# Experts' tiles laid out in pairs of one expert, with the up products made by seven half-size products

## The chip, the cores and the metric

The kernel runs on one core of one Trainium2 chip. A core has five engines with an instruction queue each: TensorE (PE; its weight loads are shown apart as PEld), VectorE (DVE), ScalarE (ACT), GpSimd (POOL) and SyncE (SP, which only issues transfers). Each engine takes its queue in order. The metric is the device time of one execution in microseconds (us), lower is better. A profiled execution has a span (from its first to its last instruction) that is a little shorter than its device time.

## The reference

A layer of gated attention and a mixture of experts over x of 2 x 2048 tokens of 512 numbers, all float32:

```python
xn = layernorm(x)
s  = attn(xn)              # causal, one head of 512, with its own norm and residual
# experts: 8, two per token, D = 512, H = 352
scores = xf @ gate_w.T + gate_b + bias
top_scores, top_idx = top_k(scores, 2)
gates = softmax(top_scores)
h = silu(einsum('td,ehd->teh', xf, w1) + b1)
y = einsum('teh,edh->ted', h, w2) + b2
out = sum over the token's two experts of gate * y
return x + s * silu(out)
```

The kernel computes an expert only for the tokens that chose it: 2 x 4096 = 8192 rows of work in all.

## The kernel before

The program has three stages, all in one order written out by hand (each engine runs its instructions in the order of the calls).

**First** (to about 258 us): the norm, the keys and values, and the routing. `route()` counts each expert's rows on DVE and gives each row a place in a list of 68 tiles of 128 rows (`NS`). The first 57 tiles (`FULL`) hold rows of one expert only; the last 11 are split into two halves of 64 rows, each of its own expert. `first`, `behind`, `end`, `jump` (L562 to L587) are the arithmetic of this layout; `toki` says which token stands in which place (L644), `posi` where a token's two rows went, `eidi` the expert of each tile or half (L663), `b1sel` its bias (L666 to L676). The pools of the expert stage are opened when `route()` has ended.

**Second** (about 259 to 599 us): the experts, one tile per call of `experts_step(i)` (L941). A tile i passes through these calls, spread over several steps so that each has time:

- `gather` (L773): POOL issues an indirect transfer of the tile's 128 rows from DRAM (`xs`), five tiles ahead.
- `turn` (L842): SP issues a transfer that transposes them (`xhT`), three tiles ahead; `join` (L847): DVE puts the two 16-bit halves of each number together again (`xT`), one tile ahead.
- `up` (L881): PE multiplies by w1 of the tile's expert; the expert's number is read into a PE register. Four products over the four chunks of D, each 128 x 352; a float32 product is two records in the profile.
- `turn_h` (L895): ACT scales the result (`h`), POOL separates its halves (`hu`), SP issues the transposing transfer (`huT`).
- `join_h` (L906): DVE joins the halves (`ht`), ACT adds the bias and applies silu in three pieces. Called two steps later.
- `down` (L919): PE multiplies by w2, three products of 512 columns, called three steps later; `keep_y` (L934), one step after that: DVE copies the result out of PSUM, SP stores it (`y_d`).

For the split tiles, `copy_w1` (ACT, L867) and `copy_w2` (DVE, L872) first copy the second half's weights to `w1c` and `w2c`, since a product takes one register. From step 8 to 46, every second step also lets SP issue one of 20 transfers that the attention will need (`early`: 16 of keys, 4 of queries; L1117 to L1121), and the last of them is followed by `query_sums(0)` on POOL.

**Third** (to the end): the attention, two rows of tiles at a time where it can. There, scores and values of some pairs are already made by seven products of half-size blocks in place of eight, with sums and differences of blocks made by DVE and POOL (`fast_scores`, `values_first`, `values_next`, `values_end`). `gather_y` and `gate` (L1347) fetch the two expert rows of each token, weigh them (ACT, DVE) and apply silu (ACT). At the last step, `gate(NT - 2)` stands between `values_next` and `values_end` (L1530), and `make_ahead` (L1379) uses its result.

Of the kernel before, what the change touches and what calls it, by code (L numbers as in the profile page):

```python
# [20 lines left out]
P = 128  # L21
# [5 lines left out]
def gated_attention_moe(  # L27
# [26 lines left out]

    nc = tc.nc
# [14 lines left out]

    HALF = P // 2
    FULL = -((E * (P - 1) - 2 * NT * P) // P)
# [3 lines left out]
    assert HL < P and HL % 32 == 0 and D == 512 and TB == 512  # L76

# [367 lines left out]
    def route():  # L445

        with ExitStack() as rt:
# [28 lines left out]
            full = counting("full", NT, step=P)  # L476

# [18 lines left out]
            def best(scores, k):  # L496
# [43 lines left out]

            count = rp.tile([P, E, 1], F32, name="count")
# [4 lines left out]
            nc.vector.tensor_scalar(short, count, 1.0 - P, None, ALU.add)  # L546
# [4 lines left out]
            halves = rp.tile([P, 2, E, 1], F32, name="halves")  # L551
            nc.vector.tensor_reduce(halves[:, 0, :, 0], more, AX.X, ALU.add)
            nc.vector.tensor_scalar(halves[:, 0], halves[:, 0], 2.0, None, ALU.mult)
            rest = rp.tile([P, E, 1], F32, name="rest")
            nc.vector.scalar_tensor_tensor(
                rest, halves[:, 0], -float(HALF), count, ALU.mult, ALU.add
            )
            nc.vector.tensor_scalar(halves[:, 1], rest, 0.0, None, ALU.is_gt)
            nc.vector.scalar_tensor_tensor(
                halves[:, 1], rest, float(HALF), halves[:, 1], ALU.is_gt, ALU.add  # L560
            )
            behind = rp.tile([P, 2, E, 1], F32, name="behind")  # L562
            nc.vector.tensor_tensor_scan(
                behind.rearrange("p k e o -> p (k e o)"), ones[:, : 2 * E],
                halves.rearrange("p k e o -> p (k e o)"), 0.0, ALU.mult, ALU.add,
            )
            first = rp.tile([P, 2, E, 1], F32, name="first")
            nc.vector.tensor_tensor(first, behind, halves, ALU.subtract)

# [5 lines left out]
            end = rp.tile([P, E, 1], F32, name="end")  # L575
            nc.vector.tensor_scalar(end, behind[:, 0], float(HALF), None, ALU.mult)
            jump = rp.tile([P, E, 1], F32, name="jump")
            nc.vector.scalar_tensor_tensor(
                jump, first[:, 1], float(HALF), end, ALU.mult, ALU.subtract
            )  # L580
            nc.vector.tensor_tensor(
                excl, excl, cum.rearrange("p (e t) -> p e t", e=E), ALU.add
            )
            nc.vector.tensor_tensor(excl, excl, shift.to_broadcast(G), ALU.add)
            nc.vector.tensor_tensor(more, excl, end.to_broadcast(G), ALU.is_ge)
            nc.vector.tensor_tensor(more, more, jump.to_broadcast(G), ALU.mult)
            nc.vector.tensor_tensor(excl, excl, more, ALU.add)  # L587

# [264 lines left out]
    def places(i):  # L855

        if i < FULL:
            return [(slice(0, P), i)]
# [736 lines left out]
```

## Time and profile before

| | us |
|---|---|
| median of 3 runs | 1049.39 (1048.91 to 1050.32) |
| the profiled execution | 1049.65 |
| its span | 1047.9 |
| PE busy in the span | 1037.7 |
| DVE busy | 635.8 |
| POOL busy | 435.4 |
| ACT busy | 332.5 |
| mean granted TensorE clock | 1.000 |

The page of the profile gives the busy time of each engine, then the span in 40 slices, then the chain of waits that ended last, then the groups of instructions by line. In a group's row, the numbers are the count, the busy time in us and the mean of one in ns, and behind the bar the idle time of the engine just before them with what ended it. PE's records are pipelined: a record's own length includes the way through the array, so the pace of a row of products is read from the distance of their starts, as the chain of waits gives it (so many records in so many us), and not from the mean length. The timeline gives start, length, engine, line and operation of each instruction; a bracket behind it is the idle time before it and what ended it. SPq is the queue of SP's transfers, and a landing is not shown in it: it is read from the instruction that waited for it.

### The profile page before, as it was taken

Reading aid. Unit: us, or ns where it says so; the run is one execution under the profiler, and the core shown is the slowest. Engines: PE = TensorE matmul, PEld = TensorE weight load, DVE = VectorE, ACT = ScalarE, POOL = GpSimd, SP = SyncE. Lnnn points to the kernel's source line nnn. Section 1 sums busy time; section 2 is a strip of 40 time slices with the busy share of each in tenths; the row PEclk is TensorE's granted clock in tenths of the full one; section 3 lists DMA queues with packets and bytes.
Section 4 is the critical chain, followed back from the end, with each engine's and each line's share of the span. In section 5 each row is a group of like instructions: output and inputs, shape, how many; then the busy total and the mean of one; then the engine's idle time right before and its main releaser. Section 6 shows DMA issues by size and latency. Waiting matters only on the chain.

```text
span 1047.9 us, 12221 instructions
## 1 busy us (share of the span) xinstructions
PE 1037.7 (99%) x3566; PEld 617.6 (59%) x3566; DVE 635.8 (61%) x1195; ACT 332.5 (32%) x675; POOL 435.4 (42%) x469
## 2 busy tenths in 40 slices
PE   9999999999999999999999999999999999999998
PEld 5687886444555555555545446776764544447577
DVE  5787884775433333333335558787556556788676
ACT  3222222211332232223246323222334553542340
POOL 2364150003433333334332117444656777764272
PEclk9999999999999999999999999999999999999999
DMA  8699999956999999999889257635767868754361
GB/s 299 186 285 283 272 266 329 333 177 172 203 228 224 229 224 230 224 232 227 201 192 169 70 191 171 136 91 131 189 176 232 259 186 230 184 144 120 96 159 40
DMA packets 300513, 209.34 MB, mean 200 GB/s; under 512 B 234520, under 2 KB 247576, under 8 KB 299424
## 3 DMA queue, kind: packets, MB, share of 16 engines
q1 hardware_dynamic: 280960, 145.60, 57.0%
q0 software_dynamic: 10560, 35.17, 13.2%
q10 hardware_dynamic: 8928, 27.79, 7.5%
q8 instruction: 30, 0.49, 0.2%
q14 instruction: 35, 0.29, 0.1%
HBM read 92.89 MB, written 60.03 MB: 146 GB/s over the span
## 4 chain that ended last, share of the span: by engine, by line
PE 89%; DVE 3%; issue 3%; POOL 2%; ACT 1%; DMA 1%; SPq 0%; ACTq 0%; POOLq 0%; DVEq 0%
PE py L928 16%; PE ph L889 15%; PE ps L1002 13%; PE p L1245 10%; PE p L1054 8%; PE po L1197 7%; PE p L402 7%; PE pj L343 3%; PE pw L209 3%; PE pj L348 3%; PE p L1197 2%; DMA zuT<-zu 1%; ACT w1c L870 1%; PE pg L309 1%; POOL xs L775 1%
## 5 line engine op out<-in xcount | busy, mean ns | idle before, releaser
L928 PE MATMUL py<-w,ht 128*128 (+3 forms) x408 | 186.6, 593 | 0.0
L889 PE MATMUL ph<-w,xT 128*128 (+1 forms) x544 | 173.1, 460 | 0.7 <-POOL keep L1111 0.7
L936 DVE COPY y<-py 128x512 f32<-128x512 f32 x68 | 46.9, 690 | 177.4 <-PE py L928 173.8
L914 ACT ACTIVATE ht<-ht,b1sel 128x128 f32<-128x128 f32 (+3 forms) x237 | 73.1, 375 | 222.3 <-DVE ht L908 220.3
L1002 PE MATMUL ps<-k,q 128*128 128x512 f32 (+3 forms) x416 | 143.0, 495 | 0.0
L889 PEld LDWEIGHTS ph<-w,xT 128*128 128x128 f32 (+1 forms) x544 | 97.4, 181 | 74.1 <-issue 35.2
L899 POOL COPY hu<-h 128x704 uint16<-128x704 uint16 x68 | 52.6, 773 | 203.4 <-ACT h L897 111.4
L1157 POOL COPY pu<-pT 128x1024 uint16<-128x1024 uint16 (+2 forms) x74 | 82.1, 1141 | 117.0 <-ACT pT L1147 53.4
L928 PEld LDWEIGHTS py<-w,ht 128*128 128x128 f32 (+3 forms) x408 | 73.6, 182 | 78.0 <-issue 39.3
L1002 PEld LDWEIGHTS ps<-k,q 128*128 128x128 f32 x416 | 74.7, 190 | 67.6 <-issue 58.6
L775 POOL DMA_INDIRECT xs<-zu_d,toki x68 | 68.9, 1013 | 69.3 <-DVE toki L644 57.9
L1342 POOL DMA_INDIRECT yg<-y_d,posi x64 | 68.3, 1067 | 38.1 <-DVE yg L1353 22.7
L1197 PE MATMUL po<-v,pT 128*128 128x512 f32 x182 | 81.1, 592 | 0.0
L266 POOL COPY zu<-z 128x1024 uint16<-128x1024 uint16 x32 | 35.2, 1100 | 78.3 <-DVE z L251 78.3
L1179 DVE COPY pT<-puT 128x1024 uint16<-128x1024 uint16 (+2 forms) x74 | 55.0, 774 | 6.1 <-DMA puT<-pu 6.1
L1197 PEld LDWEIGHTS po<-v,pT 128*128 128x128 f32 x182 | 34.2, 190 | 38.1 <-issue 36.4
L415 DVE TENSOR_TENSOR so<-p,so 128x512 f32<-128x512 f32 x70 | 45.8, 685 | 15.7 <-DMA v_d<-so 9.3
L849 DVE COPY xT<-xhT 128x1024 uint16<-128x1024 uint16 x68 | 47.4, 697 | 10.5 <-PE ph L889 5.8
L1147 ACT ACTIVATE pT<-pT,nm 128x1024 f32<-128x1024 f32 x14 | 16.1, 1149 | 111.3 <-DVE nm L1090 72.2
L1363 DVE SCALAR_TENSOR_TENSOR o<-xo,xscale,o 128x512 f32<-128x512 f32 x30 | 28.8, 967 | 33.2 <-ACT o L1360 32.0
L1147 ACT ACTIVATE pT<-ps,nm 128x512 f32<-128x512 f32 (+3 forms) x52 | 30.0, 581 | 58.8 <-DVE nm L1090 36.7
L1060 DVE TENSOR_TENSOR pT<-p,pT 128x512 f32<-128x512 f32 x49 | 32.9, 686 | 25.9 <-PE p L1054 18.7
(248 smaller groups left out, 1713.2 us busy)
## 6 DMA issues: line engine op xcount, KB each, us to landing
y_d<-y SPq DMA_DIRECT2D x68, 256.0 KB
zu_d<-zu SPq DMA_DIRECT2D x32, 264.0 KB
kt_d<-kT ACTq DMA_DIRECT2D x8, 1024.0 KB
k<-kt_d SPq DMA_DIRECT2D x32, 256.0 KB
q<-qt_d SPq DMA_DIRECT2D x32, 256.0 KB
v<-v_d SPq DMA_DIRECT2D x32, 256.0 KB
xo<-in_x_dram SPq DMA_DIRECT2D x32, 256.0 KB
x<-in_x_dram SPq DMA_DIRECT2D x30, 256.0 KB
```

Source lines behind the costliest of these rows:

```text
L402: nc.tensor.matmul(ps[:, r, :], lhsT=lhs[:, c, ts(r, P)], rhs=rhs[:, c, :], start=(c == 0), stop=(c == 1),)
L775: nc.gpsimd.indirect_dma_start(out=xs, out_offset=None, in_=zu_d, in_offset=bass.IndirectOffsetOnAxis(ap=toki[:, i : i + 1], axis=0),)
L889: nc.tensor.matmul(ph[at, :], lhsT=xT[:, c, at], rhs=rhs[k], start=(c == 0), stop=(c == ND - 1),)
L914: nc.scalar.activation(ht[:hn, c, at], ht[:hn, c, at], AF.Silu, bias=b1sel[:hn, c, j : j + 1])
L928: nc.tensor.matmul(py[at, :], lhsT=ht[:k, c, at], rhs=rhs[n], start=(c == 0), stop=(c == NH - 1),)
L1002: nc.tensor.matmul(ps[:, :w], lhsT=aqs[seq[s] // 2][:, c, ts(t % 2, P)], rhs=aks[first + j][:, c, :w], start=(c == 0), stop=(c == ND - 1),)
L1054: nc.tensor.matmul(ps, lhsT=x[:, c], rhs=y[:, c], start=(c == 0), stop=(c == ND // 2 - 1))
L1157: nc.gpsimd.tensor_copy(pu[:, : 2 * w].rearrange("p (h d) -> p h d", h=2), turned[s][:, k : k + w].bitcast(U16).rearrange("p (d h) -> p h ...
L1179: nc.vector.tensor_copy(turned[s][:, k : k + w].bitcast(U16).rearrange("p (i t h) -> p i t h", t=P, h=2), puT[:, : 2 * w // P, :].rearrang ...
L1197: nc.tensor.matmul(dst, lhsT=turned[s][:, ts(k, P)], rhs=avs[first + k // BT][:, k % BT, cols], start=(start and k == k0), stop=(k == k1 - 1),
L1245: nc.tensor.matmul(dst, lhsT=a[:, k], rhs=v(k), start=(k == 0), stop=(stop and k == n - 1))
L1342: nc.gpsimd.indirect_dma_start(out=y, out_offset=None, in_=y_d, in_offset=bass.IndirectOffsetOnAxis(ap=posi[k][:, n : n + 1], axis=0),)
```

## The change

**The layout.** An expert's rows are first cut into pairs of full tiles, then into single full tiles, then into at most one or two halves. The numbers of each are fixed: 26 pairs (52 tiles), 60 full tiles in all in place of 57, 8 split tiles in place of 11, 68 tiles as before. `route()` works with three kinds (pairs, whole tiles, halves) where it had two.

```diff
-    FULL = -((E * (P - 1) - 2 * NT * P) // P)
+    PAIRS = (2 * NT * P - E * 3 * HALF) // (2 * P)
+    FULL = (2 * NT * P - E * HALF) // P
...
+    AHEAD_OF_PAIRS = 6
+    order = list(range(2 * PAIRS, 2 * PAIRS + AHEAD_OF_PAIRS)) + list(range(2 * PAIRS))
+    order += list(range(len(order), NS))
+    paired = range(AHEAD_OF_PAIRS, AHEAD_OF_PAIRS + 2 * PAIRS)
...
+            full2 = counting("full2", NT // 2, step=2 * P)
...
+            later = [more, sc2]
+            for k, past in enumerate(later):
+                nc.vector.tensor_tensor(past, excl, end[:, k].to_broadcast(G), ALU.is_ge)
+                nc.vector.tensor_tensor(past, past, jump[:, k].to_broadcast(G), ALU.mult)
+            for past in later:
+                nc.vector.tensor_tensor(excl, excl, past, ALU.add)
...
-            for k in range(2):
+            for k in range(3):
                 nc.vector.tensor_tensor(
                     ge, half.unsqueeze(1).to_broadcast(GS), first[:, k].to_broadcast(GS), ALU.is_ge
                 )
                 n = rp.tile([P, NJ], F32, name=f"begun{k}")
                 over_e(n, ge, ALU.add)
...
+            eid = begun[0]
+            for n in begun[1:]:
+                nc.vector.scalar_tensor_tensor(eid, n, 0.0, eid, ALU.is_equal, ALU.mult)
+                nc.vector.tensor_tensor(eid, eid, n, ALU.add)
```

Steps 0 to 5 run six single full tiles; steps 6 to 57 are 26 calls of `pair_step`; steps 58 and 59 are full tiles, 60 to 67 the split ones.

**The sums.** `w1_sums` makes four differences of blocks of w1 (176 columns by half of D) for all experts, two experts at a time after each of the steps 1 to 4: three on DVE, one on POOL, 704 numbers per partition each. `x_sums` makes the four sums of a pair's rows on DVE, 256 numbers each.

**The products.** `up_pair` makes the pair's `h` (256 x 352) from seven products of 128 x 176, each over two chunks of 128, with seven additions on DVE that read the products from PSUM, and one copy by ACT.

```diff
+    def w1_sums(e, parts):
...
+        for i, x1, x2 in (1, b12, b11), (2, b22, t[0]), (3, b22, b12), (4, b21, t[1]):
+            if i in parts:
+                engine = nc.gpsimd if i == 3 else nc.vector
+                engine.tensor_tensor(t[i - 1], x1, x2, ALU.subtract)
...
+    def x_sums(i):
+        q = wsp.tile([P, 3, ND // 2, P], F32, name=f"xs4_{i}", tag="xs4")
...
+        for dst, x1, x2, op_ in (
+            (s1, a21, a22, ALU.add), (a21, a11, a21, ALU.subtract),
+            (s2, s1, a11, ALU.subtract), (s4, a12, s2, ALU.subtract),
+        ):
+            nc.vector.tensor_tensor(dst, x1, x2, op_)
...
+        def made(x, y):
+            ps = ps_a.tile([P, TB], F32, name="p7", tag="a")[:, :H2]
+            for c in range(ND // 2):
+                nc.tensor.matmul(
+                    ps, lhsT=x[:, c], rhs=y(c).rearrange("p o h -> p (o h)"),
+                    start=(c == 0), stop=(c == ND // 2 - 1),
+                )
+            return ps
...
+        nc.scalar.copy(c11, made(a11, b(0, 0)))
+        meanwhile()
+        p2 = made(a12, b(1, 0))
+        add(c12, made(s2, t(2)), c11)
+        add(c11, p2, c11)
+        add(c21, made(s3, t(3)), c12)
+        p5 = made(s1, t(1))
+        add(c22, p5, c21)
+        add(c12, p5, c12)
+        add(c12, made(s4, b(1, 1)), c12)
+        add(c21, made(a22, t(4)), c21)
```

**The steps.** A pair's step does two tiles' work in one order; `keep_y`'s copies go to ACT there. `turn_h` of a paired tile scales `h` where it lies.

```diff
+    def pair_step(i):
+        keep_y(i - DOWN - 1, nc.scalar.copy)
+        gather(i + FIRST)
+        turn(i + 3)
+        turn(i + 4)
+        up_pair(i, lambda: join_h(i - 2))
+        turn_h(i)
+        gather(i + FIRST + 1)
+        turn_h(i + 1)
+        join_h(i - 1)
+        down(i - DOWN)
+        keep_y(i - DOWN, nc.scalar.copy)
+        down(i - DOWN + 1)
+        for k in range(i + 2, i + 4):
+            join(k)
+        if i + 2 in paired:
+            x_sums(i + 2)
```

In `experts_step`, which the other tiles keep, `copy_w1` is called before `turn_h` and not after it, and for split tiles `join_h` after `turn_h` and not before `up`:

```diff
-        at(join, 1)
-        at(join_h, -2)
+        if i + 1 not in xts:
+            at(join, 1)
+        if i < FULL:
+            at(join_h, -2)
         at(up, 0)
+        at(copy_w1, 1)
         at(turn_h, 0)
-        at(copy_w1, 1)
+        if i >= FULL:
+            at(join_h, -2)
         at(down, -DOWN)
```

**Pools and transfers.** The sums' memory (`wsp`) lies where the attention's keys and queries, `w1c` and `w2c` come later; these pools are opened at step 58. So the 20 early transfers are issued two at a time after the steps 58 to 67. The two PSUM pools are opened so that a tile waits only for the former user of its own place. `xT` has four buffers and `h` four (two each before).

```diff
-    ps_b = psum(att, name="ps_b", bufs=3)
-    ps_a = psum(att, name="ps_a", bufs=5)
+    ps_b = psum(att, name="ps_b", bufs=3, reuse_waits="tile")
+    ps_a = psum(att, name="ps_a", bufs=5, reuse_waits="tile")
...
-        if i >= 8 and i % 2 == 0 and early:
-            f, b, c = early.pop(0)
-            f(b, c)
-            if not early:
-                query_sums(0, nc.gpsimd)
+        if i < paired.start:
+            if 0 < i <= E // 2:
+                w1_sums(2 * (i - 1), (1, 2, 3, 4))
+            if i + 1 == paired.start:
+                join(i + 2)
+                x_sums(i + 1)
+        for _ in range(2):
+            if i >= paired.stop and early:
+                f, b, c = early.pop(0)
+                f(b, c)
+                if not early:
+                    query_sums(0, nc.gpsimd)
```

**The end.** At the last step of the attention, `gate` is moved into `values_end`, behind its joins and sums:

```diff
             values_next(s - 3)
-            gate(s - 1)
             values_end(
-                s - 3, [lambda: join_p(s)] * len(halves[s]) + [lambda: combine_p(s - 1)]
+                s - 3,
+                [lambda: join_p(s)] * len(halves[s])
+                + [lambda: combine_p(s - 1), lambda: gate(s - 1)],
             )
```

## The prediction

> **What bounds the kernel now.** I read the page's busy times first, then the chain of waits, then the timeline and the window table of the expert stage, since the change lies there.
>
> ```profile
> PE 1037.7 (99%) x3566; PEld 617.6 (59%) x3566; DVE 635.8 (61%) x1195; ACT 332.5 (32%) x675; POOL 435.4 (42%) x469
> ```
>
> PE is busy throughout at full clock, so work taken from PE is worth its time unless something else comes due. The chain of waits (start, length, what) through full tiles:
>
> ```profile
> 301.13 2.37 PE ph L889 x8
> 303.50 2.58 PE py L928 x6
> 306.08 2.37 PE ph L889 x8
> ```
>
> Nothing but products: 2.37 us for up (8 records of 352 columns, 0.2956 each) and 2.58 for down, 4.945 us a tile. The split tiles are different:
>
> ```profile
> 563.57 0.53 ACT h L897
> 564.10 1.26 ACT w1c L870
> 565.41 2.29 PE ph L889 x13
> ```
>
> Here ACT's copy of the second expert's weights, queued behind silu and `h`, ends last before each up. A step takes up to 5.4 us.
>
> **Pairs: PE.** Two ups cost 16 x 0.2956 = 4.73 us. A pair's seven products are 7 x 2 chunks x 2 records = 28 records of 176 columns. No row has 176. The pace is 0.2956 at 352 columns (above) and 0.216 at 256 (12 records in 2.59 us, line L1245 of the chain). Both fit columns x 0.833 ns + 2.3 ns, so 176 give 0.149. This needs the weight loads to keep up:
>
> ```profile
> 785.56 0.86 PEld L1002 LDWEIGHTS ps<-k,q 128*128 128x128 f32 x7 [0.24 <-issue]
> ```
>
> That is PE's loads ahead of products with only 128 columns. A load is 190 ns long, but seven start within 0.86 us, (0.86 - 0.19) / 6 = 0.112 each: they overlap. So 0.149 stands (bounds 0.149 and 0.190): 28 x 0.149 = 4.17, 0.556 less per pair, **26 x 0.556 = -14.5 us**. A pair's step is then 4.17 + 2 x 2.58 = 9.33 us.
>
> The Trainium skill (TensorE: Matmul & The Clock Gate, section "LDWEIGHTS") gives a load as its columns / 1.2 ns, 107 ns for 128. By that figure the loads need 3.0 us a pair and products decide; by the recorded 190 ns they would need 5.32 us and the change would lose. The measured pace of 0.112 is on the page's side.
>
> **Pairs: the others in 9.33 us.** DVE: two joins 0.70, two of `ht` 0.56, seven additions from PSUM (256 columns take 0.42 us, 128 take 0.29: 0.34), four sums of 256 columns (0.42): 1.40 + 1.12 + 2.38 + 1.68 = 6.6 us. ACT: two result copies 0.585 (row L353, same shape), the first product's copy 0.35, two `h` 0.53, two silus 0.98: 4.5. POOL: two gathers 1.1 and two `hu` 0.77: 3.7. SP: four transposes 1.3, two stores 0.5: 6.2. All fit. PSUM has five places for products; the sixth product needs the first's, which ACT has long copied.
>
> DVE and POOL get in each other's way, however. Alone, the sum of query blocks on L1023 takes 0.41 us; its mean is higher:
>
> ```profile
> L1023 DVE TENSOR_TENSOR sq<-q 128x256 f32<-128x256 f32 x5 | 5.3, 1057 | 0.0
> ```
>
> The long ones lie beside POOL copies or sums. The Trainium skill (SBUF — State Buffer, section "SBUF: two separate sides") has it that a DVE operation with two SBUF inputs and a POOL operation that reads SBUF take turns on one shared pair of ports, the later one waiting for the whole of the other. By that rule the two `hu` copies cost DVE up to 1.5 us a pair, 8.1 in all. From the rows alone I add nothing here and keep the long sums for a rival.
>
> Transfers: the pair moves what two tiles moved. In the windows of 0.2 us between 500 and 505 us the DMA engines are well below full in about six of 25, so a tile needs some 3.8 us of them, 7.7 a pair.
>
> **The loop through the transpose.** What could come due is a ring. DVE's `join_h(i-2)` stands ahead of the pair's additions and waits for `huT`, which left after the former pair's additions:
>
> ```profile
> 262.39 0.77 POOL L899 COPY hu<-h 128x704 uint16<-128x704 uint16 x1 [2.26 <-ACT h L897]
> 263.19 1.21 SPq L903 DMA_TRANSPOSE huT<-hu  x1
> ...
> 267.57 0.56 DVE L908 COPY ht<-huT 128x768 uint16<-128x768 uint16 x1 [2.77 <-DMA huT<-hu]
> ```
>
> From SP's issue to DVE it took 4.4 us. Around the ring: join 0.56, six additions 2.2, `h` 0.53, `hu` 0.77, transfer 4.4, hand-overs 0.3 = 8.8 us, 0.6 below 9.33. I take no stall; the other end is one blocked POOL copy and a transfer 0.5 later, 9.9. Every 0.1 us beyond 9.33 costs 2.6 us in all.
>
> **The split stage.** Eleven steps run from 533.55 to 592.17, 58.6 us. After: three full ones (14.8), three at 5.2 as the first three in the chain (where 64- and 128-row tiles alternate), five at 4.95, since the weight copy now starts at the end of up and needs 0.24 + 1.36 us while down takes 2.58: 54.8 to 55.2. **-3.4** (other end -1.2: only three splits less at 0.38). Silu, now behind `h`, ends about 4.1 us after up; down needs it at 4.95.
>
> The 20 early transfers move here, two a step, on SP behind `huT` and ahead of the next step's store and transpose: SP 3.2 + 2 x 0.57 = 4.3 of 5 us. At the 390 GB/s that some windows of 0.2 us show, 0.5 MB take 1.3 us, which the one step's lead of the joins covers; without it, silu's margin of 0.8 is gone. The query transfers of step 66 leave some 4.5 us after up(66), and the first scores start 7.6 after it (2.58 + 2.37 + 2.58); three us for landing leave nothing. **+0.5** (0 to 2). `query_sums(0)` moves on POOL from step 46 to 67, needed 20 us later, free.
>
> **The start.** `route()` gains ten small DVE operations before L604, 2.7 us; DVE then waits 2.5 us at 210 us for PE, which has other products to run, so nothing comes of it. After `toki` a third comparison (0.8 + 1.2) and two more steps for `eid` (0.24 each) add 2.4 us to what ends here:
>
> ```profile
> 249.87 2.33 DVE L673 SCALAR_TENSOR_TENSOR b1sel<-ge,b1s,b1sel 128x79 f32<-128x79 f32 x7
> ...
> 255.80 0.69 DVE L849 COPY xT<-xhT 128x1024 uint16<-128x1024 uint16 x1 [3.61 <-DMA xhT<-xs]
> ```
>
> SP's first transpose starts at 252.42, right behind it. The first `xT` would be there at 258.9 and not 256.5. PE's former products end at 258.36, and today up starts at 259.08 (after ACT's last copy out of PSUM, 258.98, which the finer PSUM waits remove): 0 (-0.5 to +1).
>
> `w1_sums` put 3 x 0.89 = 2.7 us (704 columns at 1.04 ns + 0.15) on DVE in each of four steps that hold 1.95 us already, 4.6 of 4.95, and a POOL difference of 1.9 us (L1371: 1.39 at 512) that DVE takes turns with. `join` is queued behind. By hand I get 0.4 us late at up(4) and 0.6 at the first `x_sums`; with each POOL operation blocking DVE once, about 1 us more in two or three steps. **+3** (1 to 6).
>
> **The end.**
>
> ```profile
> 1011.73 3.85 DVE L1353 SCALAR_TENSOR_TENSOR yg<-yg,share,yg 128x512 f32<-128x512 f32 x2 [4.23 <-DMA yg<-y_d,posi]
> ...
> 1015.96 2.86 PE L1245 MATMUL p<-vT,pT 128*128 128x256 f32 x12 [1.40 <-DVE u L1262]
> ```
>
> DVE waits in `gate` for rows from DRAM, and PE for the additions behind it. Moved, PE loses its 1.40 us wait. `make_ahead` and what follows on DVE come 2 to 3 us later; the additions at 1033.97 then run at about 1036.5, before PE needs them (1039.38, now 1038). **-1.4** (0 to -1.4).
>
> **Sum:** -14.5 - 3.4 + 0.5 + 3 - 1.4 = -15.8. The span 1047.9 becomes 1032.1; with 1.75 us around it 1033.9; the runs' median lies 0.26 below the profiled execution: 1033.6, I say **1033.5 us**.
>
> **Rivals.** *The ring decides.* For it: 0.6 us of slack only, and it keeps its delay once late. Against: the 4.4 us were taken with gathers in the way already. At 9.65 a pair, 26 x 0.32 = +8.3: about 1042 us.
>
> *DVE becomes the bound*, the slower side. Place: the pair's four sums and two joins beside POOL. If each sum takes the 1.4 us of the long ones (the median on L1022 and L1023), DVE needs 6.6 + 3.9 = 10.5 us a pair: 26 x 1.17 = +30, 1064 us. It costs the whole gain from 9.33 + 15.8 / 26 = 9.94 us on. Against: POOL reads SBUF for only 1.5 us a pair.
>
> *The loads don't overlap enough* and the pair saves nothing on PE: 28 x 0.190 = 5.32 in place of 4.17, 26 x 1.15 = +30, 1063 us. It loses from 0.1689 us a record (4.73 / 28), set the other terms aside. Against: 0.112 above.
>
> **Chances.** What the kernel's runs can tell from no change is about 0.2%, 2 us. Pairs bound by products (1030 to 1038): 0.60. The ring between 9.4 and 9.9 (1038 to 1047): 0.22. DVE as the bound: 0.11. Loads: 0.03. No difference by an accident of sizes: 0.03. Below 1030: 0.01. So faster 0.83, same 0.03, slower 0.14. Range 1029.5 to 1045: the forecast's terms at their kinder ends, and most of the ring's case.
>
> **What would show it.** Right: in the chain a pair as 28 records in 4.17 us and twice 2.58, without DVE, ACT or a transfer between. The ring: DVE's `ht` row idle on `huT`, then PE idle on DVE's additions. DVE as bound: its busy share near 1 there, the sums' mean above 0.9 us. Loads: records 0.17 to 0.19 apart with no wait named. The start: PE waiting for `xT` or the sums between 268 and 284 us. The splits: `w1c` gone from the chain. The end: no PE wait of 1.4 us near 1015. I am wrong altogether if a pair takes more than 9.94 us.

## The result, and the profile after

| | before | after |
|---|---|---|
| runs | 14 | 14 |
| median, us | 1049.21 | 1055.12 |
| shortest to longest, us | 1047.6 to 1052.4 | 1042.8 to 1068.0 |
| the profiled execution, us | 1049.65 | 1049.76 |
| its span, us | 1047.9 | 1048.1 |

The ratio after to before is 1.000, with a 95% interval of 0.998 to 1.002: no difference, where 1033.5 us had been forecast. The ratio leaves out runs more than 1.5% above a kernel's shortest one, here six of the fourteen, all above 1058 us; as these may well be this kernel's own, medians and extremes of all runs stand beside the ratios below. The profiled execution is one of the shorter runs, 5.4 us under the median; what is read from its trace explains that run.

The page's busy times say that the change did remove PE's work, and that the time didn't follow:

```profile
PE 1027.8 (98%) x3836; PEld 643.9 (61%) x3836; DVE 735.2 (70%) x1449; ACT 367.2 (35%) x741; POOL 461.7 (44%) x474
```

PE is busy for 9.9 us less in a span that is 0.2 us longer: it waits for 10 us more than before. The chain of waits through the first pairs shows both sides of it (start, length, what):

```profile
299.49 1.16 DVE ht L1005
300.66 1.18 DVE xT L875
...
303.87 3.25 PE p L968 x20
307.12 5.15 PE py L1025 x12
312.27 4.18 PE p L968 x28
316.45 5.16 PE py L1025 x12
```

Where nothing holds it, a pair is what was forecast: 28 records in 4.18 us, down in 5.16. Up to the second pair (303.87) the chain isn't on PE at all but goes through a landing and DVE's joins. The table of PE's waits in the expert stage (for whom, us in total, times, longest):

```profile
PE p L968 <- DVE xs L949: 2.5, 5, 1.0
PE ph L915 <- DVE xT L875: 2.3, 2, 1.8
PE ph L915 <- issue: 2.1, 1, 2.1
PE p L968 <- DVE h L975: 0.9, 2, 0.6
PE ps L1122 <- DMA q<-qt_d: 0.8, 1, 0.8
PE p L968 <- DVE xT L875: 0.4, 1, 0.4
```

Before, the same table has a single row, 0.7 us ahead of up(0). And DVE, which PE waits for, waits itself, in the pairs from 300 to 540 us, for the transposing transfers:

```profile
DVE ht L1005 <- DMA huT<-hu: 24.6, 22, 2.5
DVE xT L875 <- DMA xhT<-xs: 19.3, 17, 2.9
```

Set side by side from one marked point to the next, the two profiled executions differ like this:

| stretch | before, us | after, us | difference | forecast |
|---|---|---|---|---|
| to the last copy of the projections (ACT, 258.39 and 262.64) | | | +4.25 | 0 |
| from there to up(0) (259.08 and 264.67) | 0.69 | 2.03 | +1.3 | start: +3 |
| up(0) to the seventh tile (281.19 and 291.80) | 22.1 | 27.1 | +5.0 | (in the +3) |
| the next 52 tiles, which are the pairs now (to 538.77 and 540.45) | 257.6 | 248.65 | -8.9 | -14.5 |
| the rest to the first scores (592.10 and 592.04) | 53.3 | 51.6 | -1.7 | -2.9 |
| to the end of the span | 455.8 | 456.1 | +0.3 | -1.4 |
| sum | | | +0.2 | -15.8 |

The first row I take as not the change's: PE waits there for `zT`, before the routing, 1.9 us in the profile before and 4.1 after, and in the profiles of the kernels below that pause was anything up to 4.2 us, whatever they changed behind it. The others are the change's.

**The start.** Timelines of SP, DVE, PE and POOL:

```profile
258.99 6.77 SPq L870 DMA_TRANSPOSE xhT<-xs  x4
...
263.77 1.37 DVE L875 COPY xT<-xhT 128x1024 uint16<-128x1024 uint16 x2 [5.00 <-DMA xhT<-xs]
...
264.67 11.40 PE L915 MATMUL ph<-w,xT 128*128 x32 [2.06 <-issue]
...
277.59 2.30 POOL L938 TENSOR_TENSOR w1s<-w 128x704 f32<-128x704 f32 x1
...
278.28 2.15 DVE L875 COPY xT<-xhT 128x1024 uint16<-128x1024 uint16 x1
...
280.49 2.63 PE L915 MATMUL ph<-w,xT 128*128 x8 [1.85 <-DVE xT L875]
```

SP's first transpose leaves at 258.99, right behind the routing's last DVE operation, though its gather was issued at 243; then PE's first up waits. In the steps with sums of weights, `join` (0.69 us alone) takes 2.15 beside POOL's difference, and up waits for it: 1.85 us here, and the two steps behind take 5.65 us each, not 4.95.

**The pairs.** The timeline where the ring is set back:

```profile
380.34 5.87 SPq L870 DMA_TRANSPOSE xhT<-xs  x2
...
383.12 0.77 POOL L996 COPY hu<-h 128x704 uint16<-128x704 uint16 x1 [4.09 <-issue]
...
385.35 0.89 DVE L1005 COPY ht<-huT 128x768 uint16<-128x768 uint16 x1 [2.54 <-DMA huT<-hu]
386.17 0.68 DVE L875 COPY xT<-xhT 128x1024 uint16<-128x1024 uint16 x1
386.26 2.71 SPq L1000 DMA_TRANSPOSE huT<-hu  x2
...
389.30 0.86 PE L968 MATMUL p<-w1s,xs 128*128 x4 [0.51 <-DVE xs L949]
...
390.26 4.07 SPq L870 DMA_TRANSPOSE xhT<-xs  x2
...
391.65 0.56 DVE L1005 COPY ht<-huT 128x768 uint16<-128x768 uint16 x1 [1.95 <-DMA huT<-hu]
392.12 2.34 DVE L975 TENSOR_TENSOR h<-p,h 128x176 f32<-128x176 f32 x7
...
392.51 0.86 PE L968 MATMUL p<-w1s,xT 128*128 x4 [0.56 <-DVE h L975]
```

Two xhT transposes hold SP for 5.87 us; huT, queued behind them, leaves at 386.26 although `hu` was ready at 383.9, and DVE joins it at 391.65, 7.8 us after `hu`. DVE waits for `huT` ahead of the joins and of the seven additions, and PE waits for both. In the next pair the same order starts late.

**The end.** The timelines of DVE and PE:

```profile
1025.35 1.41 DVE L1490 SCALAR_TENSOR_TENSOR yg<-yg,share,yg 128x512 f32<-128x512 f32 x2
...
1033.30 0.42 DVE L1399 TENSOR_TENSOR o<-p,p 128x256 f32<-128x256 f32 x1
...
1033.78 1.99 PE L1334 MATMUL p<-v,pT 128*128 128x256 f32 x8 [1.67 <-DVE o L1399]
```

PE's wait of 1.40 us at 1015.96 is gone. A new one of 1.67 has come at 1032: PSUM has three places for these products, and the one that PE needs next comes free with an addition that now stands behind the gate and `make_ahead` on DVE.

### The profile page after: what moved, and what is told of

The parts are those of the page before. It is cut to its first block, busy times and chain, and to the rows that moved or that the text cites. A ratio compares the mean times of both kernels' runs of the same rounds, so it can differ in the third digit from the quotient of the medians.

```text
span 1048.1 us, 13294 instructions
## 1 busy us (share of the span) xinstructions
PE 1027.8 (98%) x3836; PEld 643.9 (61%) x3836; DVE 735.2 (70%) x1449; ACT 367.2 (35%) x741; POOL 461.7 (44%) x474
## 4 chain that ended last, share of the span: by engine, by line
PE 73%; issue 8%; POOL 7%; DMA 7%; DVE 4%; SPq 1%; ACT 0%; POOLq 0%; DVEq 0%
PE ps L1122 13%; PE py L1025 9%; PE p L1174 8%; PE p L1382 8%; PE p L412 8%; PE po L1334 7%; PE p L968 7%; PE pj L353 3%; PE pw L219 3%; PE pj L358 3%; PE p L1334 2%; POOL xs L801 2%; DMA huT<-hu 2%; POOL hu L996 1%; DMA zuT<-zu 1%
## 5 line engine op out<-in xcount | busy, mean ns | idle before, releaser
L1025 PE MATMUL py<-w,ht 128*128 (+3 forms) x408 | 182.2, 593 | 0.0
L996 POOL COPY hu<-h 128x704 uint16<-128x704 uint16 x68 | 63.7, 937 | 175.1 <-issue 129.6
L801 POOL DMA_INDIRECT xs<-zu_d,toki x68 | 75.1, 1105 | 69.5 <-DVE toki L669 57.8
L875 DVE COPY xT<-xhT 128x1024 uint16<-128x1024 uint16 x68 | 61.8, 916 | 25.2 <-DMA xhT<-xs 25.0
L975 DVE TENSOR_TENSOR h<-p,h 128x176 f32<-128x176 f32 x182 | 56.1, 337 | 15.2 <-PE p L968 8.0
L1005 DVE COPY ht<-huT 128x768 uint16<-128x768 uint16 x68 | 40.3, 592 | 33.2 <-DMA huT<-hu 31.4
L1508 POOL TENSOR_TENSOR o<-o,yg 128x512 f32<-128x512 f32 x30 | 41.4, 1381 | 14.9 <-DVE o L1500 14.7
```

The lines of the kernel that those rows point to most:

```text
L801: nc.gpsimd.indirect_dma_start(out=xs, out_offset=None, in_=zu_d, in_offset=bass.IndirectOffsetOnAxis(ap=toki[:, order[i] : order[i] + 1], ...
L996: nc.gpsimd.tensor_copy(hu[:, :, :H], h.bitcast(U16).rearrange("p (d h) -> p h d", h=2))
L1025: nc.tensor.matmul(py[at, :], lhsT=ht[:k, c, at], rhs=rhs[n], start=(c == 0), stop=(c == NH - 1),)
```

## The experiments

Sixteen kernels. Each line of times is the median of all runs of that kernel (shortest to longest), then the ratio to the kernel before with its interval.

**1. The pairs undone.** Every tile through `experts_step`; the layout, the transfers and the gate as changed.

```diff
-        h = phs[i] if i in paired else hp.tile([P, H], F32, name=f"h_{i}", tag="h", bufs=4)
+        h = hp.tile([P, H], F32, name=f"h_{i}", tag="h", bufs=4)
...
-        if i in paired:
+        if False:
             if (i - paired.start) % 2 == 0:
                 pair_step(i)
...
-            if 0 < i <= E // 2:
-                w1_sums(2 * (i - 1), (1, 2, 3, 4))
-            if i + 1 == paired.start:
-                join(i + 2)
-                x_sums(i + 1)
+            pass
```

> The pairs undone: tiles, split tiles, early transfers and gate as in the changed kernel, but all tiles go through experts_step with eight-record ups of 352 columns; neither w1_sums nor x_sums nor the additions are there. Theory (the pair step, with the sums of weights ahead of it, is where time is lost and where the runs spread): the layout alone keeps the split stage's gain of 1.7 to 3.4 us against 53.3 and loses about 1 at the start: 1046 to 1049 us, and all runs within 3 us of each other. Rival (the layout, the early transfers or the moved gate cost the time): 1052 or more, or a spread of over 10 us here too.

Measured: 1050.4 us (1048.2 to 1054.4), 0.9989 (0.9974 to 1.0004). The theory holds in kind, though its figures were missed (the median is 1.4 us above its range, the runs lie 6 us apart and not 3): the layout alone is worth between -2.7 and +0.4 us, and the spread is 6 us, as before's, not 25. The loss and the spread belong to the pairs and to what prepares them.

**2 to 4. The ring opened, first try.** In e2_deep both `join_h` stand behind the next pair's `x_sums`; e3_lead turns xhT earlier; e4_both does both.

```diff
-    DOWN = 3
+    DOWN = 4
...
-        up_pair(i, lambda: join_h(i - 2))
+        up_pair(i, lambda: None)
...
-        join_h(i - 1)
...
             x_sums(i + 2)
+        join_h(i - 2)
+        join_h(i - 1)
```

```diff
         gather(i + FIRST)
-        turn(i + 3)
         turn(i + 4)
...
         turn_h(i + 1)
+        turn(i + 5)
```

> The ring opened at huT: both join_h stand behind the next pair's x_sums on DVE and down runs a tile later (DOWN 4), so that nothing that up needs is queued behind a wait for huT. Theory A (DVE's wait for huT ahead of the additions and of x_sums holds PE): pair steps of 9.33 throughout, the 6 us of pauses between 291 and 540 us gone: 1041 to 1045 us, spread under 6 us. Theory B (it is xhT that lands late, joins wait for it themselves): DVE's wait moves from the ht row to the xT row, the time stays at 1047 to 1056. Theory C (DVE's own work with POOL beside it): no wait of PE goes, 1049 or more.

> xhT a pair step earlier: turn(i+4) at the start of a pair step, turn(i+5) behind huT(i+1), so that a join has 9 us or more from the issue in place of 4 to 5, and huT(i) has one transpose less ahead of it on SP. Theory B (late xhT holds the joins and with them x_sums): DVE's 25 us before the xT row fall under 5, pauses of PE for DVE xs gone, 1041 to 1046 us. Theory A (huT): PE's pauses for DVE stay, 1047 to 1056.

> Both: join_h behind x_sums with DOWN 4, and xhT a pair step earlier (hu buffers 3). Theories A and B together say that neither huT nor xhT ends last anywhere in the pair stage: 26 pairs of 9.33 us, 1040 to 1043 us with a spread under 5 us. If PE still waits for DVE there, or if pairs are still 9.5 us and more, the bound is DVE's own work beside POOL (theory C): 1048 or more.

Measured: e2_deep 1080.7 us (1073.9 to 1085.6), 1.028 (1.025 to 1.031); e3_lead 1047.2 (1044.7 to 1058.1), 0.9949 (0.9932 to 0.9967); e4_both 1068.5 (1066.4 to 1070.7), 1.016 (1.014 to 1.018). e2_deep and e4_both lie far above every figure but theory C's open end, and not for C's reason. PE's waits in e2_deep's pairs say why (same columns as above; in the experiments' files the lines are shifted by a few):

```profile
PE p L967 <- ACT h L976: 18.7, 22, 1.4
PE p L967 <- DVE xs L948: 4.3, 5, 1.6
```

Almost every pair waits for ACT's copy of its first product. `join_h` issues not only DVE's join but also three silus on ACT, and behind x_sums these stood ahead of that copy in ACT's queue: the wait for `huT` had only been handed to another engine. In e3_lead's profile, DVE's waits in the pairs were these:

```profile
DVE ht L1007 <- DMA huT<-hu: 44.5, 33, 4.6
...
DVE xT L877 <- DMA xhT<-xs: 1.0, 1, 1.0
```

The earlier xhT is waited for once, as theory B expected, and the median lies just above its range; yet this profiled run (1058 us) was a long one, PE waiting 5.6 us for the additions and 2.9 still for `xs`. What is left is the wait for `huT`, and it had grown from 24.6 us to 44.5.

**5 and 6. The ring opened, second try.** `join_h` is cut in two: DVE's part behind `x_sums`, the silus of the former pair behind ACT's copy of the first product.

```diff
-        up_pair(i, lambda: join_h(i - 2))
+        up_pair(i, lambda: [silu(k) for k in (i - 4, i - 3) if k not in silued])
...
             x_sums(i + 2)
+        for k in (i - 2, i - 1):
+            join_h(k, i + 2 in paired)
```

> As e2_deep (both join_h behind x_sums, DOWN 4), but the silus of those tiles stand behind ACT's copy of the next pair's first product, where e2_deep had them ahead of it. Theory (e2_deep was slow because ACT ran silu, which waits for huT through DVE, ahead of the copy that the additions wait for; the idea of keeping the wait for huT off the additions' way was not wrong): DVE's 47 us of waits for ACT's h copy go under 5, PE's 22 us for it go, and the time is 1041 to 1047 us. Rival (the delay comes through xhT and the joins as well): PE's waits for DVE xs and xT stay at 5 us or more, 1047 to 1055.

> e5_silu_behind with xhT a pair step earlier, as in e3_lead (hu buffers 3). Theory (the two transposes' landing times are all that holds the pair stage): no pause of PE over 0.3 us between the second pair and 540 us, 1039 to 1043 us, spread under 6 us. Rival (DVE with POOL beside it): pairs of over 9.5 us with DVE busy throughout, 1047 or more.

Measured: e5_silu_behind 1048.0 us (1043.8 to 1056.5), 0.9975 (0.9955 to 0.9994); e6_silu_lead 1047.5 (1044.2 to 1050.9), 0.9964 (0.9947 to 0.9982). PE waits for ACT's copy no more. But in e5_silu_behind it was the rival's figures that came true: PE waits 2.8 us for `xs` in four pairs and 4.5 us for `xT` at the start, and DVE, which now waits only 1.2 us for huT, waits 47.0 for xhT. In e6_silu_lead 23 of the last 24 pairs take 9.34 us and one 10.4; the time is still over the expected 1043, since PE waits 6.0 us for `xT` and 2.2 us for the first up at the start. Half of the theory stands (the pairs), the rest of the time is elsewhere.

**7. The sums of weights without POOL**, on top of e6_silu_lead:

```diff
-                engine = nc.gpsimd if i == 3 else nc.vector
-                engine.tensor_tensor(t[i - 1], x1, x2, ALU.subtract)
+                nc.vector.tensor_tensor(t[i - 1], x1, x2, ALU.subtract)
...
-            if 0 < i <= E // 2:
-                w1_sums(2 * (i - 1), (1, 2, 3, 4))
+            for k in range(3 * i, min(3 * i + 3, 2 * E)):
+                w1_sums(2 * (k // 4), (1 + k % 4,))
```

> e6_silu_lead with the 16 sums of weights all on DVE, three a step from step 0, none on POOL. Theory (steps 3 to 5 take 5.65 us in place of 4.95 since DVE's join takes turns with POOL's 2.3 us difference): the three steps go to 4.95 to 5.1 us, 2 to 3.5 us less than e6_silu_lead, 1036 to 1041 us. Rival (sums of 0.89 us are simply too many for DVE): DVE gets 0.89 us more a step in steps 0 to 4, joins later still, same as e6 or up to 2 us more.

Measured: 1047.5 us (1042.8 to 1055.6), 0.9973 (0.9950 to 0.9997): the median didn't move, which is the rival's figure and not the theory's 1036 to 1041. In the profile the start is shorter (25.1 us from up(0) to the first pair against 27.7 in e6_silu_lead's, waits for `xT` of 2.0 us against 6.0) and all pairs from the second on take 9.34; but of the last two steps ahead of the pairs one takes 6.7 us, as in e6_silu_lead, and only the other the expected 4.95, and PE still waits 2.5 us before the first up.

**8. The pairs as changed, without their gathers.**

```diff
     def gather(i):
+        if 11 <= i < paired.stop:
+            xss[i] = kept[0]
+            return
...
```

> The changed kernel with the gathers of tiles 11 to 57 left out: these tiles all use one kept xs, so their rows are not the reference's; everything else runs, the transposes too. Theory (the gathers' packets beside the transposes hold SP's issue and delay landing, and this starts the pauses): SP's xhT and huT rows at 1.2 to 1.3 us each without long ones, no pause of PE over 0.3 us after the third pair, pair stage 26 x 9.33 = 243 us. Rival (DVE's own work and POOL's hu copies): pauses as before, pair stage 247 us or more.

Measured: 1043.6 us (1039.9 to 1046.2), 0.992 (0.990 to 0.994). From 290 to 540 us PE has a single wait, at the first pair; the second row is DVE's waits for `huT` in the pairs:

```profile
PE p L975 <- DVE xs L956: 1.0, 1, 1.0
```

```profile
DVE ht L1012 <- DMA huT<-hu: 4.4, 7, 1.3
```

The same order of work as in the change, 25 pairs in a row at 9.34 us, 244.0 us for the pairs in place of 248.65, and 4.4 us of DVE's waits for huT where there were 24.6. So in these two profiles it takes the gathers for the ring to bite; their packets and POOL's time for them (1.1 us each) went together, and no run parts the two. SP's issues are short without them: huT's 1.22 us on the mean, longest 1.28; xhT's 1.36, longest 2.34, over the 47 tiles that use the kept `xs`. From 510 us on gathers run again, and the five xhT there take 1.5 to 4.0. (In the change xhT's mean is 2.02, with a longest of 4.43; before, 1.48 and 2.08.)

**9 and 10. The first transposes and the end**, on top of e7_sums_dve:

```diff
-        xh = xtp.tile([P, 2 * ND, P], U16, name=f"xhT_{i}", tag="xhT", bufs=4)
+        xh = xsp.tile([P, 2 * ND, P], U16, name=f"xhT_{i}", tag="xhT", bufs=4)
```

```diff
-                + [lambda: combine_p(s - 1), lambda: gate(s - 1)],
+                + [lambda: combine_p(s - 1)],
             )
+            first_sum(NT - 2)
+            gate(s - 1)
             for k in AHEAD:
                 make_ahead(k)
```

`first_sum` is the part of `values_first` up to its addition.

> e7_sums_dve with the xhT buffers in the pool of xs, which is there before the routing, so that SP's first transpose waits for its gather and no longer for the end of the routing's work, whose memory it took. Theory (up(0) is late by 2.1 to 2.5 us since the first transpose is issued at 259 us, behind DVE's last selection of b1sel): first transposes at 245 to 250 us, DVE joins at about 259, PE's pause of 2.5 us before up(0) under 0.7, granted clock 1.00 between 262 and 270 us, the first x_sums earlier too: 3 to 5 us less than e7_sums_dve, a median of 1042 to 1045. Rival (DVE, not SP, ends last there, or transfers do): the pause stays over 1.5 us and the time at 1047.

> e9_early_xht with the first addition of the last pair of blocks (values_first) ahead of the gate and of make_ahead on DVE. Theory (the moved gate only moved PE's wait: the place in PSUM that p03 needs comes free behind gate and make_ahead): PE's wait of 1.7 to 2.7 us for DVE's addition at 1025 to 1034 us goes, no other pause over 0.4 us takes its place, 1.5 to 2.7 us less than e9_early_xht. Rival (the end is a chain of DVE's work, whatever its order): PE's wait goes but the last stores end as late, less than 0.7 us.

Measured: e9_early_xht 1043.3 us (1041.6 to 1049.9), 0.9923 (0.9905 to 0.9942); e10_tail 1040.6 (1036.4 to 1045.0), 0.9906 (0.9882 to 0.9929). Both medians are about as expected; the intervals of the two overlap, so what the second edit does is read from the traces. In e9_early_xht the first up follows the last projection without a pause; the end's wait is still 2.9 us there. In e10_tail it is gone, and PE's waits over 0.4 us from the expert stage on are these, none of them in a pair but the first:

```profile
PE ph L917 <- DVE xT L877: 2.5, 3, 1.5
PE p L969 <- DVE xs L950: 2.2, 1, 2.2
PE ps L1131 <- DMA q<-qt_d: 1.2, 1, 1.2
```

**11. The pairs' worth, all else mended alike**: e1_plain with the edits of 9 and 10.

> e1_plain (no products of pairs) with the same two edits as e10_tail: xhT in the pool of xs, the addition ahead of the gate. It is e10_tail's partner, the kernels differ by the pairs and by what they need. Theory (a pair is worth 0.556 us once nothing holds it, 14.5 us in all, less 1 to 3 for the sums of weights and the first sums of rows): e10_tail 11 to 13 us below this kernel, this one at 1045 to 1049 us. Rival (the pairs give back more than half through contention): 7 us or less between them.

Measured: 1044.5 us (1043.6 to 1049.1), 0.9946 (0.9924 to 0.9967). e10_tail is 3.9 us below it by medians, 8.0 by the profiled spans (1034.7 against 1042.7, where e10_tail's is that of its shortest run): the rival's 7 us or less by the medians, and less than the theory's 11 by either. The two profiles say where it goes: e10_tail's pairs behind the first are all at 9.34 us, but before the second pair it loses some 5.6 us (the steps of the sums 3.2, the wait for the first `x_sums` 2.4), as all its sums of weights are DVE's between 257 and 280 us.

**12 to 16. What the ring costs, and what the start does.** e12_seven_ahead puts a seventh single tile ahead of the pairs, to spread the sums. e13_ring_kept has the edits of 7, 9 and 10 with the pair step of the change; e14_lead_mended adds e3_lead's earlier xhT, e15_seven_down3 the seventh tile. e16_first_steps reorders the single tiles' steps of e12_seven_ahead. First the edit of the seventh tile, then e16_first_steps':

```diff
-    AHEAD_OF_PAIRS = 6
+    AHEAD_OF_PAIRS = 7
...
-            for k in range(3 * i, min(3 * i + 3, 2 * E)):
+            for k in range((0, 2, 4, 6, 9, 12, 14)[i], (2, 4, 6, 9, 12, 14, 16)[i]):
...
-        for _ in range(2):
+        for _ in range(3):
```

```diff
+        if 0 <= i < paired.start:
+            turn(i + 4)
...
                 w1_sums(2 * (k // 4), (1 + k % 4,))
+            if i >= 2:
+                join_h(i - 2)
```

> e10_tail with seven single tiles ahead of the pairs in place of six (as many pairs as before), the 16 sums of weights two or three to a step over seven steps, and three early transfers a step in the split stage. Theory (the start loses 5.6 us since DVE, from 257 us on, does 16 sums of 0.89 us on top of 1.95 us a step): PE's waits for DVE xT and xs there, 2.5 and 2.2 us in e10_tail, fall to 1 us or less together, the wait for q under 0.5: 3 to 5 us less than e10_tail, a median of 1035.5 to 1038. Rival (what ends there last is transfers or the order of the first joins): 1 us or less.

> The changed kernel with the edits of e7_sums_dve, e9_early_xht and e10_tail (sums of weights on DVE, xhT in the pool of xs, the addition ahead of the gate), but the pair step as the change has it: both join_h where they were, DOWN 3, xhT turned at the start of the step. Its difference to e10_tail is what the pair step's order costs. Theory (the ring gives 3 to 15 us of pauses, differing from run to run): a median of 1044 to 1050 us and a spread of 8 us or more. Rival (the pair step's order hardly matters once the start is right): within 2 us of e10_tail.

> e13_ring_kept with xhT a pair step earlier, as in e3_lead; join_h and DOWN 3 stay as the change has them. Theory (in e13_ring_kept the runs from 1034 to 1054 us differ by how often late transposes set the ring back, and xhT's issue on SP is where it starts): spread under 7 us, a median of 1036 to 1040. Rival (the differences between runs come from elsewhere, the first stage's wait for zT or the start): spread and median as e13_ring_kept, 1040 to 1041.

> e14_lead_mended with seven single tiles ahead, the sums two or three to a step and three early transfers a step, as in e12_seven_ahead, but with DOWN 3. Theory (e12_seven_ahead missed since with DOWN 4 the first five ups follow each other and the fifth waits for DVE, which waits for the first huT): no wait of PE for DVE xT of over 1 us between 255 and 290 us, the first x_sums waited for under 0.3 us, 1 to 3 us below e14_lead_mended. Rival (the start is bound by DVE however the sums are spread): the same as e14_lead_mended within 1 us.

> e12_seven_ahead with two things moved in the single tiles' steps: xhT of tile i+4 is turned in step i, so that the fifth one leaves ahead of the first huT on SP, and join_h stands behind the step's sums of weights on DVE. Theory (e12_seven_ahead lost its 6.8 us at the start since the fifth xT was queued on DVE behind the wait for the first huT, and xhT behind huT on SP; the pair steps are right already): PE's waits for DVE xT between 255 and 290 us under 1.5 us, pairs at 9.34 us, no run above 1044 us, a median of 1035 to 1039. Rival (DVE's load at the start decides in any order): PE's waits there stay at 4 us or more, 1040 to 1042.

| | median, us (shortest to longest) | runs | ratio |
|---|---|---|---|
| e12_seven_ahead (ring open, xhT earlier) | 1041.9 (1034.8 to 1046.4) | 6 | 0.9895 (0.9865 to 0.9925) |
| e13_ring_kept (pair step as changed) | 1040.7 (1034.0 to 1054.3) | 6 | 0.9898 (0.9879 to 0.9917) |
| e14_lead_mended (ring closed, xhT earlier) | 1049.9 (1036.2 to 1064.5) | 12 | 0.9963 (0.9934 to 0.9992) |
| e15_seven_down3 (ring closed, xhT earlier) | 1054.9 (1040.1 to 1065.2) | 11 | 0.9973 (0.9935 to 1.0010) |
| e16_first_steps (ring open, xhT earlier) | 1039.8 (1034.1 to 1045.9) | 6 | 0.9905 (0.9869 to 0.9942) |

The cleanest pair is e12_seven_ahead and e15_seven_down3, which differ in the order of the pair step (`DOWN`, `join_h`, silu) and the buffers that go with it; both turn xhT earlier than the change does. PE's waits from 255 to 600 us, first e15_seven_down3, then e12_seven_ahead:

```profile
PE p L969 <- DVE h L976: 9.8, 7, 2.6
PE ph L917 <- DVE xT L877: 1.6, 1, 1.6
PE p L969 <- DVE xs L950: 0.9, 4, 0.3
```

```profile
PE ph L917 <- DVE xT L877: 6.8, 3, 3.0
```

With `join_h` ahead of the additions, PE waits up to 2.6 us at a time for additions that stand behind a join of `ht`; with the other order there is no wait in any pair. (The waits for `xT` lie outside the pairs, see below.) By medians of all runs it is 13 us, by the ratios 8. (The two ran beside before's medians of 1049.6 and 1051.3 us.)

That is not yet what the change's own order costs, for it turns xhT later. e13_ring_kept, which does too, has the expected spread, but its median missed the 1044 to 1050 us and is within 0.2 us of e10_tail's, as its rival said; its profiled run, 1034.0 us, is the shortest of all, with the ring closed. Six runs over 20 us decide little, but e14_lead_mended, which should have been better, was 9 us worse with twice as many (both its numbers missed). The lengths of the pair stage in the profiles, from the first pair to the next single tile (242.6 us without any wait), sort the kernels (one profile each; e3_lead's is that of its longest run):

| pair stage, us | xhT as changed | xhT a pair step earlier |
|---|---|---|
| `join_h` ahead of the additions | the change 248.7, e13_ring_kept 246.3 | e3_lead 260.4, e14_lead_mended 260.9, e15_seven_down3 259.3 |
| `join_h` behind `x_sums`, silu behind ACT's copy | e5_silu_behind 246.5 | e6_silu_lead 244.7, e7_sums_dve 243.9, e9_early_xht 243.4, e10_tail 245.1, e12_seven_ahead 242.7, e16_first_steps 244.6 |

So the two edits help together. Opened at huT alone, DVE's waits go to xhT and `x_sums` come late (e5_silu_behind); with xhT earlier alone they go to huT (44.5 us in e3_lead, 47.6 in e15_seven_down3) and the pairs lose more than in the change. Why they lose so much more is not shown. In the kernels with the ring opened so, from e5_silu_behind on, no spread is over 13 us.

For the start, e12_seven_ahead missed: one wait of 3.0 us for `xT` where 1 or less was expected, and with the lower clock behind it 4.8 us lost (29.1 us from up(0) to the first pair, where seven ups and three downs need 24.3). The other 3.9 of its 6.8 us lie in the split stage, so the expectations of e15_seven_down3 and e16_first_steps, which put all 6.8 at the start, misread them. There the early transfers, three a step now, stand ahead of xhT on SP, here for 4.0 us:

```profile
554.30 4.01 SPq L828 DMA_DIRECT2D k<-kt_d  x3
...
559.06 1.66 SPq L871 DMA_TRANSPOSE xhT<-xs  x1
...
560.75 0.70 DVE L877 COPY xT<-xhT 128x1024 uint16<-128x1024 uint16 x1 [6.44 <-DMA xhT<-xs]
...
561.50 0.51 PE L917 MATMUL ph<-w,xT 128*64 x1 [2.95 <-DVE xT L877]
```

e15_seven_down3 has 1.6 us of waits for `xT` in its split stage and e16_first_steps 1.9, where e10_tail, with two transfers a step, has none. e15_seven_down3's start was clean (no wait between 255 and 290 us; its total missed by the pairs), and e16_first_steps, which should have settled it by order alone, still shows

```profile
PE ph L917 <- DVE xT L877: 4.5, 3, 1.9
PE p L969 <- DVE xs L950: 1.7, 1, 1.7
```

of which 2.6 us for `xT` and the 1.7 at the first pair are the start's. Its rival was nearer, and with the ring open (`DOWN` 4) some 5 us stay at the start. Which of DVE's load and the first huT's landing is the limit there remains open. e10_tail, e12_seven_ahead and e16_first_steps, and e13_ring_kept with its pair step as changed, can't be told apart by their medians; all are 9.3 to 11.1 us below before's runs beside them.

## Why the prediction was wrong

Right, by its own steps:

- *Pairs, PE.* Products decide, at 0.149 us a record: 4.18 us for 28 records against 4.17. The rival "loads don't overlap" is out.
- *DVE as the bound* (1064 us) is out: no run shows DVE busy throughout a pair. Its x_sums are longer beside POOL (0.87 us on the mean for one of the four in e10_tail, 0.42 alone), but within the slack.
- *The split stage*, in kind. `w1c` has left the chain, and three of the last four steps take 4.95 us; the three put at 5.2 took 5.29, two others 5.0. The wait for the queries (0.5, 0 to 2) was 0.8 us here and between nothing and 2.4 in the experiments; -1.7 in place of -2.9.
- *The sign of being wrong altogether*, more than 9.94 us a pair, did not come: a pair took 9.56. The pairs did gain 8.9 us, and the other terms used it up.

Wrong, in the order of size in the profiled run:

- *"Around the ring: ... transfer 4.4, hand-overs 0.3 = 8.8 us, 0.6 below 9.33. I take no stall."* This step failed, by its term for the transfer. The 4.4 us from SP's issue to DVE were one landing, taken where tiles came singly; with it the ring has room for 5.0. In the changed kernel's pairs 22 joins of `ht` found DVE already waiting for them, and from the end of `hu`'s copy to these joins it took 5.8 us on the mean, 4.0 to 7.9, in 14 of the 22 more than 5.0. Two xhT transposes stand together on SP ahead of huT, beside two gathers, and hold it for up to 5.9 us. In the profiled run this was worth 4.7 us (6.0 of pauses in the pairs, less 1.3 at the first one), in e15_seven_down3, with xhT earlier, 16. The rival "the ring decides" was the true case in the pairs: its 9.65 us a pair against 248.65 / 26 = 9.56 measured.
- *The start, "+3 (1 to 6)".* The mechanism was right, the size was not: 1.3 + 5.0, and 1.3 more for the first `x_sums`, 7.6 us. For the first up, "0 (-0.5 to +1)" had the routing's 2.4 us right (SP's first transpose moved from 252.42 to 258.99, of which 4.25 are the first stage's), but counted on a landing as before: from its issue to the join 3.4 us there, 4.8 now. e9_early_xht, whose first transposes don't wait for the routing's memory, has no pause there. The sums of weights were given 0.4 and 0.6 us and about 1 in two or three steps, while the three steps behind the first four ups took 3.3 us more together; and the first four ups themselves took 1.7 more at the lower clock behind PE's pause, for which no term stood.
- *The end, -1.4.* "The additions ... would run at about 1036.5, before PE needs them" looked at the wrong addition. The one that counts is that which frees a place in PSUM, 1.67 us late. e10_tail shows it: with that addition ahead of the gate, the wait is gone.
- *What was not foreseen at all:* the first stage's 4.25 us, which differ from run to run and which I don't count as part of the change.

Put together: 3.3 + 1.3 at the start, 4.7 in the pairs less 0.45 (the last of the 52 tiles was a split one before, of 5.2 us), 1.2 in the splits, 1.7 at the end and 4.25 in the first stage are the 16.0 us between -15.8 and +0.2.

That is the profiled run. How much of the median's further 5.4 us and of the 25 us between the shortest and the longest run is the ring's isn't shown, as no run above 1058 us of this kernel was profiled; the spreads (6 us without pairs, 7 to 13 with the ring opened as from e5_silu_behind on, 13 to 28 with it closed) speak for a large part. Against the ring as the only cause stands e13_ring_kept: with the start and the end mended and the pair step as changed, its median is 1040.7 us, inside the forecast's range, and its profiled pairs lose 3.7 us. There the start and the end were worth more than the ring.

## What to carry to other kernels

A ring through a transfer (result, transfer, join, next result) must be costed with the long landings of a crowded queue, not with one measured landing: here the term of 4.4 us was 4.0 to 7.9, on a slack of 0.6. Open it by putting the wait behind the next round's work on every engine that it passes, ACT as well as DVE: handing it from one in-order queue to another (e2_deep) cost more than it saved. Look, too, at the other transfer that shares the queue: here only both edits together left the pairs without waits, and one of them alone (xhT earlier, as in e3_lead) made the profiled pairs longer. And where an instruction is moved past others, look for buffers, in PSUM above all, that the ones now behind it were to free.

## What the runs showed of the hardware

The granted clock after a pause. In the first stage PE waited 4.07 us for `zT` up to 92.27 us; the windows behind that (stretch, PE busy, records, granted clock, DMA share, GB/s):

```profile
88.00:92.00 4.00, 0.20 (x1) 0.90 0.83 260
92.00:96.00 4.00, 3.73 (x13) 0.50 0.60 232
96.00:100.00 4.00, 4.00 (x15) 0.75 1.03 329
```

Eight records that take 1.89 us at full clock took 3.78, so a pause of 4.1 us cost some 6. After the 2.06 us before up(0) the clock was 0.72 from 264 to 270 us; in e1_plain a pause of 2.1 us at the same place left it at 1.00. The Trainium skill (TensorE: Matmul & The Clock Gate, section "What's actually happening") has it that the array falls to half clock after an idle window of about 3.4 us, and that the window runs free of the program; the 0.50 agrees, the drop after 2.06 us is shorter than the window it gives, and whether the window's phase explains that it came in one kernel and not in the other, no run here tells.

SP's issue of a transpose isn't of fixed length: for xhT 1.48 us on the mean and up to 2.08 before, 2.02 and up to 4.43 in the changed pairs, 1.36 and up to 2.34 in the same pairs without gathers.
